# Three mixes of a four-layer graph network: from seven Winograd products in fp32 to three fp32r passes over split operands, with the SBUF pools laid out anew

## The chip, the cores and the metric

The kernel runs on one core of one Trainium2 chip. The metric is device time in microseconds (us) for one launch; before the change it is 946.98 us, the median of 3 runs (946.92 to 947.29).

## The reference

32 graphs of 512 nodes with 128 features pass four layers, each of the form `x = x + layer(relu(layernorm(x)), adj)`; `adj` is one 512 x 512 matrix for all graphs. Cut to what matters here:

```python
# layer 0: attention over the graph, from adj > 0 and a vector e (softmax by rows)
out = (A * I) @ (h @ W[0]) + (A * (1 - I)) @ (h @ W[1]) + bias
# layer 1: Chebyshev hops, the same matrix twice
x1 = einsum('bnf,nw->bwf', h, adj)                 # first mix
x2 = 2 * einsum('bnf,nw->bwf', x1, adj) - h        # second mix
out = relu(concat(h, x1, x2, x1, x2) @ Theta1 + bias)
# layer 2
feat = relu(h @ psi_w + psi_b)
msg = einsum('nm,bnd->bmd', adj * adj, feat)       # the mix of layer 2
out = relu(concat(msg, h) @ phi1_w + phi1_b) @ phi2_w + phi2_b
# layer 3: attention with tanh-clipped scores, masked by adj
out = (softmax-like of exp(8 * tanh(h q (h k)^T / (8 sqrt(128)))) * adj) @ h @ v
```

All arrays are fp32.

## The kernel before

**Tiling.** The work runs in pairs of graphs: q = 0 to 15 is a pair, b = 0 or 1 a graph in it, r = 0 to 7 a round of two pairs (A = 2r and C = 2r + 1). Nodes lie in four blocks of 128 (t, i), on the partitions; `xq` and `xt` keep all of x in SBUF from start to end.

**Mixes before.** A mix multiplies a 512 x 512 matrix with the 512 rows of a pair. It is done as one level of Winograd's form of Strassen's algorithm: the matrix is cut in 2 x 2 blocks of 256, and seven products of blocks (`products`, `ORDER`) take the place of eight. The sums of blocks on the matrix side are made once (`sum_steps`, on POOL); those on the data side for each pair (`right_steps`, L350 to L361: rt_h for layer 1's first mix, rt_w for its second, rt_feat for layer 2). `by_feature` (L384) gives the result with features on the partitions (layer 1's first mix x1T, layer 2's msgT), `by_token` (L391) with nodes on them (layer 0's mix and layer 1's second). Each product is 256 columns wide, in fp32; VectorE and ScalarE put the results together as they come out of PSUM (`mixed`, L402 to L424; `evict` in layer 1, L1031 to L1056).

**Layer 1, a round.** `normed` (ScalarE, L252) gives h; `transposed` (VectorE 32 x 32 transposes L288, then a bounce through DRAM, L295 and L297) gives hT; `straight` copies it into node order (hs, POOL, L739). The first mix gives x1T. Because Theta1's five blocks act on h, x1, x2, x1, x2, the kernel multiplies first and mixes after: p_w = h Th1 + x1 Th2 (`weighed`, L464, copied out as w by ScalarE at L987), then the second mix of w with adj, plus the "own" matmuls h Th0 (L797), bias, relu and the residual.

**Layer 2, a pair.** feat (L1092, L1093), the mix msgT, phi1 (L1109, L1110) with the relu at L1111, phi2 and the residual (L1115).

**Layer 3, a (q,b).** It already uses the three-pass form. A number v is split in a high part (v rounded on its way into an fp32r tile, scaled by `DOWN`), a low part (the rest, brought to scale) and a mid part made of v and high; high times high, low times low and mid times mid, each one fp32r matmul, sum up to the product at a known factor (`UP`, `LOW`). `moving_parts` splits keys (ScalarE L436, POOL L437, VectorE L438), `scaled_parts` queries (L442 to L444). Scores of 512 columns (L1155) go through tanh (L1156), exp (L1160) and the mask (L1162, VectorE and POOL by turns) into ex, and ex times hv (p_av, L1172) is scaled and added to x (L1174, L1177).

**Order.** Layer 0 (`round0`) is written out by hand in program order under `manual_schedule`. After it the layers are generators, and the loop at the end (`waiting`, `active`) interleaves them: each pass starts the next entry and takes one step of every generator that runs, the older first. From there the compiler orders each engine's instructions itself, with program order as priority. Stores and loads are issued on SP.

**Pools.** A tag is a set of buffers of equal size, and a tile waits for a free one. Before: "square" (const, 4 of 8 KB a partition: adj, att, attT, later x1T, sq, the mask adjTx and three ex), "sums" (2), and in `work` "rt" (6), "u" (3), "quad" (2), "hT" (4), "h" (3), and "hs" (6, in `late`); layers 0 to 3 share them by turns. In layer 3 keys take "hs" and "u", queries "rt", ex "square", and qkh with hv "quad".

Of the kernel before, what the change touches and what calls it, by code (L numbers as in the profile page):

```python
# [17 lines left out]
P = 128  # L18
QR = 32
# [10 lines left out]
def kernel(  # L30
# [48 lines left out]
    work = ctx.enter_context(tc.tile_pool(name="work", bufs=4))  # L79
    bounce = ctx.enter_context(tc.tile_pool(name="bounce", bufs=4, space=bass.MemoryType.DRAM))  # L80
# [11 lines left out]
    def square_tile(name):  # L92
        return const.tile([P, NT, N], F32, tag="square", name=name, bufs=4)
# [13 lines left out]
    adj_s = square_tile("adj_s")  # L107
# [198 lines left out]
    def sum_steps(mat, name, eng=nc.gpsimd):  # L306

        a11, a12 = mat[:, 0:2, 0:H], mat[:, 2:4, 0:H]
        a21, a22 = mat[:, 0:2, H:N], mat[:, 2:4, H:N]
        extra = const.tile([P, 3, 2, H], F32, tag="sums", name=f"sums_{name}", bufs=2)  # L310
        s1, s2, s4 = extra[:, 0], extra[:, 1], extra[:, 2]
        sums[name] = {1: a11, 2: a12, 3: s4, 4: a22, 5: s1, 6: s2, 7: a21}
        for out, op, p, q in ((s1, OP.add, a21, a22), (s2, OP.subtract, s1, a11),
                              (a21, OP.subtract, a11, a21), (s4, OP.subtract, a12, s2)):
            tc.keep_in_program_order(eng.tensor_tensor(out, p, q, op))
            yield

# [5 lines left out]
    def att_sums():  # L323
# [3 lines left out]
        extra = const.tile([P, 3, 2, H], F32, tag="sums", name="sums_att", bufs=2)  # L327
# [15 lines left out]
    def right_blocks(half, name, engs):  # L343

        right = {}
        for _ in right_steps(half, name, engs, right):
            pass
        return right

    def right_steps(half, name, engs, right):  # L350
        b11, b12, b21, b22 = half(0, 0), half(0, 1), half(1, 0), half(1, 1)
        if len(b11.shape) == 4:
            t = [work.tile([P, 2, 2, D], F32, tag="rt", name=f"rt_{name}_{i}", bufs=6) for i in range(4)]
        else:
            t = []
            for i in range(2):
                two = work.tile([P, 2, 2, D], F32, tag="rt", name=f"rt_{name}_{i}", bufs=6)
                t += [two[:, 0], two[:, 1]]
        right.update({1: b11, 2: b21, 3: b22, 4: t[3], 5: t[0], 6: t[1], 7: t[2]})
        for i, (p, q) in enumerate(((b12, b11), (b22, t[0]), (b22, b12), (b21, t[1]))):  # L360
            engs[i].tensor_sub(t[i], p, q)  # L361
            yield
# [18 lines left out]
    def by_feature(p, a, b, first):  # L381

        for k in range(2):
            nc.tensor.matmul(p[:, :H], b[:, k, :], a[:, k, :], start=(first and k == 0),  # L384
                             stop=(k == 1), skip_group_check=True)

# [8 lines left out]
    def u_tile(name):  # L395
        return work.tile([P, 2, H], F32, tag="u", name=f"u_{name}", bufs=3)

    def mixed(name, left, right, dst):

        m1 = dst[:, 0, H:], dst[:, 1, :H], dst[:, 1, H:]  # L400

        def evict(k, p):  # L402
            p = p[:, :H]
            if k == 1:
                nc.scalar.copy(m1[0], p)
            elif k == 6:
                nc.vector.tensor_add(m1[1], p, m1[0])
            elif k == 7:
                nc.vector.tensor_add(m1[2], p, m1[0])
            elif k == 5:  # L410
                return
            elif k == 2:
                nc.scalar.copy(dst[:, 0, :H], p)
            elif k == 4:
                nc.vector.tensor_add(dst[:, 0, H:], p, m1[0])
            elif k == 3:
                nc.vector.tensor_add(dst[:, 1, :H], p, m1[1])

        def evict2(k, p):
            evict(k, p)  # L420
            if k == 5:
                held.append(p)
            if k == 7:
                nc.vector.tensor_add(dst[:, 1, H:], held[0][:, :H], m1[2])  # L424

        held = []
        return products(name, by_feature, left, right, evict2)
# [40 lines left out]
    def quad_tile(name):  # L468
        return work.tile([P, 2, 2 * N + 2 * NT], F32, tag="quad", name=name, bufs=2)
# [8 lines left out]
    def project_steps(q, hT, copy=nc.scalar.copy):  # L478
        r, w = divmod(q, 2)
        if w == 0:  # L480
            if r % 3 == 2:
                g[r] = square_tile(f"g_{r}").rearrange("p t (b w f) -> p t b w f", b=2, w=2)
            else:
                t = quad_tile(f"g_{r}").rearrange("p w e -> p (w e)")[:, : 4 * N]
# [243 lines left out]
    late = ctx.enter_context(tc.tile_pool(name="late", bufs=4))  # L728
    for _ in range(NQ // 4, NQ // 2 - 1):
# [4 lines left out]
    def straight(hT, b, scale, name):  # L734

        s = late.tile([P, N], F32, tag="hs", name=name, bufs=6)
        src = hT[:, :, b, :].rearrange("p b (a c) -> p a b c", c=QR)
        if scale is None:
            nc.gpsimd.tensor_copy(split(s), src)  # L739
        else:  # L740
            nc.gpsimd.tensor_mul(split(s), src, split(scale))
# [8 lines left out]
    def late_sums():  # L750

        yield from sum_steps(adj_s, "adj")


        for out, op, p, q in ((1, OP.add, 1, 3), (2, OP.add, 2, 4), (0, OP.subtract, 0, 2)):
            tc.keep_in_program_order(nc.gpsimd.tensor_tensor(th[:, out, :], th[:, p, :], th[:, q, :], op))
            yield
        tc.keep_in_program_order(nc.gpsimd.tensor_scalar(th[:, 2, :], th[:, 2, :], 2.0, None, OP.mult))
# [493 lines left out]
```

## Time and profile before

| what | value |
|---|---|
| median of 3 runs | 946.98 us (946.92 to 947.29) |
| the profiled execution, its own time | 946.18 us |
| its span, from the first to the last instruction | 944.4 us |
| granted TensorE clock | 1.00 of full speed |
| DMA | 86.08 MB, mean 91 GB/s |

The profile is one execution. PE is TensorE's matmuls, PEld its weight loads, DVE VectorE, ACT ScalarE, POOL GpSimd, SP the queue that issues nearly all DMAs. A row of groups gives line, engine, operation, tiles and shapes, count, busy time and mean ns; a row of the timeline gives the start, the length, engine, line, tiles, count, and in brackets the idle time before it with what ended it. An fp32 matmul has two records. Ends of matmuls are modelled, so the distance between starts tells what one costs.

### The profile page before, as it was taken

The page shows a single profiled execution, that of the slowest core. Times are in us where ns is not written, and L with a number is a line of the kernel's source. Part 1 is how long each engine was busy: PE and PEld are TensorE (multiplying, and loading weights), DVE is VectorE, ACT ScalarE, POOL GpSimd, SP SyncE. Part 2 cuts the span into 40 slices and gives each one's busy share as a digit, 9 for nine tenths or more (in the row PEclk, how much of TensorE's full clock was granted, in tenths as well). Part 3 has the DMA queues.
Part 4 walks back from the last instruction along what each step waited for, and adds up shares of the span by engine and source line. Part 5 has one row for each costly group of instructions (what it writes and reads, how often), then busy time and mean ns, then how long its engine had stood idle before and what let it go on. Part 6 is the DMA issues. An engine that isn't in the chain of part 4 may idle for free. (4 is left out here: it accounts for less than half of the span.)

```text
span 944.4 us, 15678 instructions
## 1 busy us (share of the span) xinstructions
PE 929.0 (98%) x5625; PEld 811.2 (86%) x5625; DVE 685.4 (73%) x1390; ACT 499.1 (53%) x1120; POOL 543.8 (58%) x536
## 2 busy tenths in 40 slices
PE   8999999999999999999999999999989999999997
PEld 4899999899999999899977787778779899999996
DVE  8888885745555545556667766565699999999995
ACT  5864451451241242365734855545677666666663
POOL 5878997933428524421624334433467878787873
PEclk9999999999999999999999999999999999999999
DMA  9256533242341311424333342223223121212111
GB/s 260 58 157 193 166 112 90 72 131 67 87 122 60 90 32 59 134 67 112 90 112 86 93 128 77 86 68 90 67 60 98 57 79 57 79 57 78 34 35 44
DMA packets 83916, 86.08 MB, mean 91 GB/s; under 512 B 6784, under 2 KB 74624, under 8 KB 83840
## 3 DMA queue, kind: packets, MB, share of 16 engines
q1 hardware_dynamic: 83552, 84.57, 31.8%
q8 instruction: 44, 0.72, 0.3%
q10 hardware_dynamic: 288, 0.52, 0.1%
q14 instruction: 32, 0.26, 0.1%
HBM read 44.17 MB, written 40.89 MB: 90 GB/s over the span
## 5 line engine op out<-in xcount | busy, mean ns | idle before, releaser
L252 ACT ACTIVATE h<-x,sh,rs 128x128 f32<-128x128 f32 x512 | 209.5, 485 | 46.6 <-PE p_x1T_d L384 21.6
L1172 PE MATMUL p_av<-qkh_hv,ex 128*128 128x129 f32 x1024 | 121.8, 276 | 3.2 <-POOL ex L1162 2.2
L1172 PEld LDWEIGHTS p_av<-qkh_hv,ex 128*128 128x128 f32 x1024 | 119.1, 191 | 6.2 <-POOL ex L1162 3.0
L1162 POOL TENSOR_TENSOR ex<-ex,adjTx 128x512 f32<-128x512 f32 x62 | 105.0, 1713 | 6.7 <-issue 5.7
L1162 DVE TENSOR_TENSOR ex<-ex,adjTx 128x512 f32<-128x512 f32 x66 | 87.5, 1331 | 18.4 <-ACT ex L1160 18.4
L288 DVE STREAM_TRANSPOSE hb_hT<-h 128x512 f32<-128x512 f32 x120 | 82.0, 697 | 24.2 <-ACT h L252 23.9
L232 DVE BATCH_NORM_STATS2 bn<-x 128x6 f32<-128x256 f32 x248 | 89.5, 417 | 0.5
L361 POOL TENSOR_TENSOR rt_w<-w,rt_w 128x512 f32<-128x512 f32 x16 | 20.4, 1273 | 110.3 <-DVE rt_w L361 92.0
L361 POOL TENSOR_TENSOR rt_feat<-feat,feat 128x256 f32<-128x256 f32 x16 | 11.6, 725 | 119.4 <-ACT feat L1093 119.4
L1156 ACT ACTIVATE ex<-p_score 128x512 f32<-128x512 f32 x128 | 69.7, 591 | 17.7 <-PE p_score L1155 17.6
L987 ACT COPY w<-p_w 128x512 f32<-128x512 f32 x32 | 18.2, 574 | 106.1 <-PE p_w L464 106.1
L1160 ACT ACTIVATE ex<-ex 128x512 f32<-128x512 f32 x128 | 73.2, 638 | 0.8
L437 POOL TENSOR_TENSOR key_low<-hT,key_high 128x512 fp32r<-128x512 f32 x32 | 54.5, 1702 | 32.2 <-ACT key_high L436 29.7
L444 POOL TENSOR_TENSOR query_mid<-query_high,query_low 128x512 fp32r<-128x512 f32 x32 | 41.2, 1288 | 41.5 <-PE p_qkh L1139 22.2
L442 ACT ACTIVATE query_high<-qkh_hv 128x512 fp32r<-128x512 f32 x32 | 20.2, 633 | 65.0 <-DVE qkh_hv L1142 64.2
L1155 PE MATMUL p_score<-query_high,key_high 128*128 128x512 f32 x128 | 52.4, 417 | 1.9 <-ACT query_high L442 1.9
L1155 PE MATMUL p_score<-query_mid,key_mid 128*128 128x512 f32 x128 | 50.2, 396 | 0.8 <-POOL query_mid L444 0.8
L464 PE MATMUL p_w<-th,hs 128*128 128x128 f32 x256 | 49.5, 275 | 0.0
L464 PE MATMUL p_w<-th,x1T 128*128 128x128 f32 x256 | 49.5, 275 | 0.0
L1155 PE MATMUL p_score<-query_low,key_low 128*128 128x512 f32 x128 | 49.4, 390 | 0.0
L1104 POOL TENSOR_TENSOR x<-x,phi2b 128x256 f32<-128x256 f32 x64 | 45.0, 732 | 0.0
L1093 ACT ACTIVATE feat<-feat 128x512 f32<-128x512 f32 x32 | 20.1, 629 | 41.1 <-DVE feat L1092 41.1
(256 smaller groups left out, 2373.1 us busy)
## 6 DMA issues: line engine op xcount, KB each, us to landing
d_hT<-hb_hT SPq DMA_DIRECT2D x240, 128.0 KB
hT<-d_hT SPq DMA_DIRECT2D x60, 512.0 KB
x<-in_x_dram SPq DMA_DIRECT2D x32, 256.0 KB
out_dram<-x SPq DMA_DIRECT2D x31, 256.0 KB
adjT_d<-adj_squares SPq DMA_DIRECT2D x4, 256.0 KB
sq<-in_adj_dram SPq DMA_DIRECT2D x4, 256.0 KB
adjTx<-adjT_d SPq DMA_DIRECT2D x4, 256.0 KB
adj_s<-in_adj_dram ACTq DMA_DIRECT2D x2, 256.0 KB
```

The source lines that it names most:

```text
L232: nc.vector.bn_stats(st[:, k].rearrange("p e s -> p (e s)"), xt[q][:, b, t : t + 2, :].rearrange("p t f -> p f t"))
L252: nc.scalar.activation(h[:, b, t, :], xt[q][:, b, t, :], AF.Relu, bias=shift[q][:, i : i + 1], scale=scale[q][:, i : i + 1])
L288: nc.vector.transpose(hb[:, :, b].rearrange("p j t r -> p t j r"), h[:, b].rearrange("p t (j c) -> p t j c", c=QR))
L437: nc.gpsimd.tensor_sub(low, x, high.bitcast(F32))
L444: nc.gpsimd.tensor_sub(mid, high.bitcast(F32), low.bitcast(F32))
L464: nc.tensor.matmul(p[:, blk(t)], hT(t), w, start=(i == 0), stop=(i == len(terms) - 1))
L1104: tc.keep_in_program_order(nc.gpsimd.tensor_add(xi, xi, spread(phi2b, 2)))
L1155: nc.tensor.matmul(ps, keys[b][i][:, t, :], query[i], start=(i == 0), stop=(i == 2))
L1156: nc.scalar.activation(ex[:, t, :], ps, AF.Tanh, scale=UP / (8.0 * math.sqrt(D)))
L1160: nc.scalar.activation(ex[:, t, :], ex[:, t, :], AF.Exp, scale=8.0)
L1162: eng.tensor_mul(split(ex[:, t, :]), split(ex[:, t, :]), crossed(adjTx[0][:, t, :]))
L1172: nc.tensor.matmul(po[:, i, : D + 1], ex[:, t, blk(i0 + i)], hv[:, t, :], start=(t == 0), stop=(t == NT - 1))
```

## The change

The three mixes (layer 1's two and layer 2's) no longer use seven products of blocks. Both operands are split in high, low and mid, as layer 3 does, and a mix of one graph (512 columns) is 3 parts x 4 node blocks = 12 fp32r matmuls of 512 columns in one PSUM bank. `sum_steps`, `right_blocks`, `by_feature` and `mixed` are gone; layer 0's mix stays as it was.

- adj is split once, during layer 0 (`late_parts`, ScalarE and POOL); adj * adj is split on POOL during layer 1 (`square`), starting one entry of `waiting` sooner; the mask's load (`load_mask`) moves from there to the end of layer 2.
- h is split for the first mix (`split_up`), w as it leaves PSUM (`weighed`: ScalarE high, VectorE low and mid), feat for layer 2's mix. The results leave PSUM in one ScalarE copy each (`mixed_parts`).
- The second mix takes one bank per node block i: four own matmuls per bank, then the 12, then two VectorE instructions.
- Pools: layer 0's square, rt, u, quad and sums tiles lie in a pool of their own ("early"), the hd tiles in "owns"; both are closed after layer 0, and a pool "after" takes their room, with six "wide" tiles (8 KB a partition) and eleven "small" ones (2 KB). w1's three parts, the parts of adj * adj, msgT, and in layer 3 the keys (three parts in one), ex and values are wide; parts of h and feat, x1T, y, qkh and query parts are small. adj and its parts, later the mask, have a tag "matrix" of three. hs moves into the tag "hT" (4).

```diff
+    early_scope = ExitStack()
+    region0 = early_scope.enter_context(tc.tile_pool(name="early", bufs=2, side="right"))
...
+    def matrix_tile(name, dtype=F32):
+        return const.tile([P, NT, N], dtype, tag="matrix", name=name, bufs=3)
+
+    def wide_tile(name, dtype=F32):
+        return after.tile([P, 4, N], dtype, tag="wide", name=name, bufs=6)
+
+    def small_tile(name, dtype=F32):
+        return after.tile([P, N], dtype, tag="small", name=name, bufs=11)
...
+    def mixed_parts(name, left, right, dst):
+
+        p = bank(f"p_{name}")
+        for part in range(3):
+            for t in range(NT):
+                nc.tensor.matmul(p, right[part][:, blk(t)], left[part][:, t, :],
+                                 start=(t == 0 and part == 0), stop=(t == NT - 1 and part == 2))
+        nc.scalar.activation(dst, p, AF.Copy, scale=UP)
+
+    def three(name):
+        return [small_tile(f"{part}_{name}", F32R) for part in PARTS]
...
+    def late_parts():
+
+        adj_parts.extend(matrix_tile(f"adj_{part}", F32R) for part in PARTS[:2])
+        high, low = adj_parts
+        for t in range(NT):
+            nc.scalar.activation(high[:, t, :], adj_s[:, t, :], AF.Copy, scale=DOWN)
+            tc.keep_in_program_order(nc.gpsimd.tensor_sub(adj_s[:, t, :], adj_s[:, t, :], high[:, t, :].bitcast(F32)))
+            yield
...
+        nc.gpsimd.tensor_scalar(th[:, 0, :], th[:, 0, :], 1.0 / UP, None, OP.mult)
+        for t in range(NT):
+            nc.scalar.activation(low[:, t, :], adj_s[:, t, :], AF.Copy, scale=LOW)
+        yield
+        adj_parts.append(matrix_tile(f"adj_{PARTS[2]}", F32R))
...
+            hT[q] = work.tile([P, 2, N], F32, tag="hT", name=f"hs_{q}", bufs=4)
...
+        def split_up(q):
+            for b in range(2):
+                parts[q, b] = three(f"h_{q}_{b}")
+                moving_parts(h[q][:, b].rearrange("p t f -> p (t f)"), *parts[q, b])
 
         def first(q):
-            for _ in mixed(f"x1T_{q}", sums["adj"], right[q], x1T(q)):
-                pass
             for b in range(2):
-                hs[q, b] = straight(hT[q], b, None, f"hs_{q}_{b}")
+                x1[q, b] = small_tile(f"x1T_{q}_{b}")
+                mixed_parts(f"x1T_{q}_{b}", adj_parts, parts[q, b], x1[q, b])
...
         def weighed(q):
             for b in range(2):
-                p = projected(f"p_w_{q}_{b}", (columns(hs[q, b]), th[:, 1, :]), (columns(x1T(q)[:, b]), th[:, 2, :]))
-                nc.scalar.copy(w1[:, :, b, q % 2, :], p)
+                j = 2 * (q % 2) + b
+                p = projected(f"p_w_{q}_{b}", (rows(q, b), th[:, 1, :]), (columns(x1[q, b]), th[:, 2, :]))
+                high, low, mid = (tiles_of(part)[:, :, j, :] for part in w1)
+                nc.scalar.activation(high, p, AF.Copy, scale=DOWN)
+                nc.vector.tensor_sub(low, p, high.bitcast(F32))
+                nc.vector.scalar_tensor_tensor(mid, p, 1.0 / UP, high.bitcast(F32), OP.mult, OP.subtract)
...
+        w1 = [wide_tile(f"w_{part}_{r}", F32R) for part in PARTS]
...
+        for i in range(NT):
+            p = bank(f"p_l1_{r}_{i}")
+            for j in range(4):
+                nc.tensor.matmul(p[:, blk(j)], rows(2 * r + j // 2, j % 2)(i), th[:, 0, :],
+                                 start=(j == 0), stop=False, skip_group_check=True)
+            for part in range(3):
+                for t in range(NT):
+                    nc.tensor.matmul(p, adj_parts[part][:, t, blk(i)], w1[part][:, t, :],
+                                     start=False, stop=(part == 2 and t == NT - 1), skip_group_check=True)
+            y = small_tile(f"y_{r}_{i}")
+            nc.vector.scalar_tensor_tensor(tiles(y), tiles(p), UP, spread(b1, 4), OP.mult, OP.add)
+            x = xq[r].rearrange("p w b t f -> p (w b) t f")[:, :, i, :]
+            nc.vector.scalar_tensor_tensor(x, tiles(y), 0.0, x, OP.max, OP.add)
...
-        right = right_blocks(lambda J, b: feat[b][:, 2 * J : 2 * J + 2, :], f"feat_{q}", [nc.gpsimd] * 4)
+        right = [three(f"feat_{q}_{b}") for b in range(2)]
+        for b in range(2):
+            moving_parts(feat[b], *right[b])
...
-            keys[b] = [late.tile([P, NQR, P], F32R, tag="hs", name=f"key_{part}_{q}_{b}", bufs=6) for part in PARTS[:2]]
-            keys[b].append(work.tile([P, NQR, P], F32R, tag="u", name=f"key_{PARTS[2]}_{q}_{b}", bufs=3))
+            both = wide_tile(f"key_{q}_{b}", F32R)
+            keys[b] = [both[:, i].rearrange("p (t n) -> p t n", t=NQR) for i in range(3)]
...
-            ex = square_tile(f"ex_{q}_{b}")
+            ex = wide_tile(f"ex_{q}_{b}")
...
+            nc.gpsimd.tensor_mul(row, row, row)
+            nc.gpsimd.tensor_scalar(split(high), crossed(row), DOWN, 1.0, OP.mult, OP.mult)
+            yield
+            nc.gpsimd.tensor_sub(crossed(row), crossed(row), split(high.bitcast(F32)))
+            nc.gpsimd.tensor_scalar(split(low), crossed(row), LOW, 1.0, OP.mult, OP.mult)
+            yield
...
+    own_scope.close()
+    early_scope.close()
+    after = ctx.enter_context(tc.tile_pool(name="after", bufs=6, side="right", reuse_waits="tile"))
...
-    waiting[5].append(square())
+    waiting[4].append(square())
...
+    waiting[-2].append(load_mask())
```

## The prediction

> **What bounds the kernel now.** I read the page first: the busy line, the slices, the groups; then the stretches by layer, then TensorE's timeline.
>
> ```profile
> span 944.4 us, 15678 instructions
> PE 929.0 (98%) x5625; PEld 811.2 (86%) x5625; DVE 685.4 (73%) x1390; ACT 499.1 (53%) x1120; POOL 543.8 (58%) x536
> 0.00:180.00 180.00, 174.92 (x1089) 154.06 (x1090) 144.76 (x337) 97.63 (x240) 143.71 (x150) 1.00 0.50 137
> 180.00:460.00 280.00, 279.12 (x1666) 254.29 (x1666) 159.18 (x331) 110.90 (x279) 116.42 (x139) 1.00 0.33 90
> 460.00:680.00 220.00, 219.46 (x1117) 170.00 (x1117) 143.15 (x299) 115.50 (x269) 90.26 (x126) 1.00 0.32 92
> 680.00:944.00 264.00, 255.46 (x1757) 232.80 (x1756) 238.31 (x425) 175.09 (x334) 193.38 (x122) 1.00 0.20 61
> ```
>
> The four stretches are about layers 0, 1, 2 and 3 (columns: stretch, length, then PE, PEld, DVE, ACT, POOL). TensorE is full in all; in layers 1 and 2 nothing else passes 65%, in layer 3 VectorE has 238 of 264 us. Since ends of matmuls are modelled, I took starts:
>
> ```profile
> 203.22 1.03 PE L384 MATMUL p_x1T_a<-adj_s,h 128*128 128x256 f32 x4
> ...
> 209.26 1.89 PE L391 MATMUL p_l_a<-w,adj_s 128*128 128x256 f32 x8
> ...
> 775.32 3.74 PE L1172 MATMUL p_av<-qkh_hv,ex 128*128 128x129 f32 x32
> 778.82 0.47 PE L1155 MATMUL p_score<-query_high,key_high 128*128 128x512 f32 x1
> 779.13 0.39 PE L1155 MATMUL p_score<-query_low,key_low 128*128 128x512 f32 x1
> ...
> 781.44 0.40 PE L1155 MATMUL p_score<-query_mid,key_mid 128*128 128x512 f32 x1
> ```
>
> One whole mix (7 products x 4 records = 28) takes 209.26 - 203.22 = 6.04 us, 0.2157 per record of 256 columns; an fp32 matmul is two such records. In layer 3 the fp32r matmul of 512 columns is one record and starts every (781.44 - 779.13)/10 = 0.231 us; ten in an earlier run (771.23 to 773.50) give 0.227. With such spacings I laid the matmuls end to end: outside the first 20 us the gaps come to less than 21 us in all, about half of them at 680-760 and after 920. So the kernel lasts as long as TensorE's list, and a change is worth what it takes from that list, unless a wait appears.
>
> [...]2 x 0.2157 = 0.431 us for 256 columns against 0.229 for 512, a ratio of 3.8 per column. [...]key_mid on VectorE took 0.68 us at 777.00 and 1.76 at 783.93.
>
> **The change part by part.**
>
> *Matmuls.* Removed: layer 1's first mix, its second, layer 2's mix, 448 records each (the groups at L384 and L391 on adj_s, sq and their sums): 1344 x 0.2157 = 289.9 us. Added: 3 mixes x 16 pairs x 24 matmuls of 512 columns = 1152 at 0.229 = 263.8. Net -26.1 us; with 0.227 -28.4, with 0.231 -23.8. The "own" matmuls (16 of 128 columns a round) and the projections stay. All of it lies on the path.
>
> *Other engines in layers 1 and 2*, per pair. POOL, layer 1: loses four rt_h subtractions (0.75) and half of three rt_w (1.27), gains two subtractions for the low part (1.28, the query_mid row): 4.9 becomes 2.6; the two copies (0.77) stay. VectorE, layer 1: loses five adds of 0.42, half of the second mix's eviction (twelve instructions of 0.67 to 0.79 and an rt_w, 9.2 us a round); gains two key_mid-like instructions (1.14), two low at 0.69, two mid about 0.75 and half of eight evictions (0.75): 6.7 becomes 8.2. ScalarE gains two 0.63 and 0.43 of eviction. Layer 2: VectorE +0.2, ScalarE +1.7, POOL -0.4. A pair lasts about 16 us in layer 1 and 13.3 in layer 2; all lies beside the matmuls. Price 0. The cover is the next pair's mix (5.5 us) and the own matmuls (3.6): without it the chain high, low, mid behind p_w (0.57 + 0.69 + 0.75 = 2 us) would stand 8 times, 16 us.
>
> *Squares.* POOL's work on sq grows from 12.4 us to 4 x (1.15 + 1.58 + 1.70 + 1.58) + 4 x 1.27 = 29, spread over nine steps of layer 1, where POOL has 164 us idle: 0. The mask's load leaves that place for the end of layer 2: its four issues held SP 11.5 us (250.14), ahead of hT loads that layer 3 needs only steps later: 0. Three w1 parts, the raw square and two sq parts fill the six "wide" buffers, so w1 is single from there; its writers wait for the end of the last second mix, and p_w and the next first mix stand between: 0.
>
> *Layer 0.* The halves of adj cost ScalarE 5 us and POOL 8 x 1.28 + 2.3 = 12.5 against 7.0. POOL is at 16.4 to 18.1 of 20 us there; I take +1 (0 to 4).
>
> *Layer 0 to 1.* The first split of h goes into memory that layer 0 still uses, and TensorE waits for high (0.63) and then low (1.28), where rt_h lay ready. +2 (0 to 5; no gain, as nothing on this path gets shorter).
>
> *Layer 2 to 3.* The three parts of sq hold three of six wide buffers until the last layer-2 mix; keys of pair 1, now split at 660, wait for them. +2 (0 to 6).
>
> *Layer 3.* Same work, less memory. Keys (3 sets in tags "hs" and "u"), ex (3 in "square") and values (2 in "quad") had eight places; now six shared. How places are given the trace shows:
>
> ```profile
> 281.12 1.28 POOL L361 TENSOR_TENSOR rt_w<-w,rt_w 128x512 f32<-128x512 f32 x1 [17.94 <-DVE rt_w L361]
> ...
> 286.64 0.72 POOL L361 TENSOR_TENSOR rt_h<-h 128x256 f32<-128x256 f32 x1 [1.79 <-PE p_l_d L391]
> ...
> 290.39 0.68 DVE L1048 TENSOR_TENSOR y<-p_l_b,u_l 128x512 f32<-128x512 f32 x1
> ```
>
> The first rt_w place is free when product 6 ends (284.67), and POOL at 284.86, yet rt_h waits for product 5: the first place was kept for y, earlier in the program, which is written only at 290.39. So within a tag places go in program order. Per step of two (q,b) the program asks for ex(n), values, ex(n+1), key, key. Counting those alive, ex(n) gets its place only when the av of n-1 has ended (freeing ex and values), where now tanh runs 10 to 14 us ahead of that (779.8 against 793.8). The loop is then: tanh x4 2.06, exp x4 2.21 (rows at 680.58, 682.50), the same for n+1, two query highs 1.26, POOL's pair of multiplies (3.44, row at 778.78), which can start behind the second exp and so ends 2.3 after the fourth, av 3.50, five handovers of 0.1 (rt_h above began 0.08 after the end of its product, 284.67 + 1.89): 16.1 us. Behind a waiting tanh on ScalarE stand its exps and the next pairs' key and query highs; the multiplies on VectorE and POOL wait for it, and p_av for those. TensorE's own list per step is 2 x (0.69 + 0.85 + 2.77 + 3.55) = 15.7, and the measured period is 15.9 (key_high at 776.27 and 792.16). So the spare is gone: 16.1 bare, and VectorE, 15.3 busy of 15.9, must hit each handover. I take 16.5: 14 steps x 0.6 = +8. Bounds: -4 (the gaps it has now vanish) to 14 x 2.6 = +36 (a period of 18.5).
>
> *Sum.* -26.1 + 1 + 2 + 2 + 8 = -13.1 us. Against the profiled execution (946.18 us for a span of 944.4, 1.8 around it) that is 933.1; the median of the runs, 946.98, lies 0.8 higher: **934**.
>
> **Rivals.**
> *A, the whole gain.* Program order is overtaken where it matters (the scores of n run into PSUM ahead, as they can with eight banks), layer 3 keeps 15.9: -26.1 + 3 = 924. For it: TensorE's list in layer 3 is unchanged and its gaps small. Against: keys always fill their three places today. 0.27.
> *B, slower: six places for three kinds of tile in layer 3.* ex and its av alternate instead of overlapping, and TensorE waits for tanh, exp and the multiplies in each step. It decides from a period of 15.9 + 21.1/14 = 17.4 us; at 18.5 the sum is 947 - 21.1 + 36 = 962; with no overlap at all (tanh, exp, tail, av = 10.1, with three handovers 10.4 per (q,b) against 7.95) 32 x 2.45 = +78, 1004. For it: VectorE's 96% leaves no slack. 0.30.
> *C, no change*: a period near 17.4. 0.07.
> *D, that the passes are dearer elsewhere than in the scores*: from 0.25 us per matmul the gain is gone. Against: same form, new weights each time there too, other engines busier. Inside the range, no chance of its own.
>
> **How the numbers follow.** Forecast (928 to 942) 0.36, A 0.27, B 0.30, C 0.07. Faster by over 0.2% (1.9 us, about what a measurement here can tell from none): 0.36 + 0.27 = 0.63; within: 0.07; slower: 0.30. Range: below, A with the cheaper matmul and half of its three small costs, 947 - 28.4 + 1.5 = 920; above, B at 18.5 with the upper ends of the other costs in part, 966. About 0.05 lies below, 0.13 above. As both signs hold much: the forecast's own range is 928 to 942.
>
> **What would show it.** fp32r matmuls of both mixes 0.227 to 0.231 us apart (right), 0.25 (D). Layers 1 and 2 end some 21 to 26 us earlier; gaps between p_w and the second mix would show the 2 us cover missing. Layer 3's period from one av to the next but one: 15.9 (A), 16.5 (forecast), over 17.4 (B); in B TensorE idles before p_av on ex, and ScalarE's tanh starts when the av before it ends. The forecast is wrong if tanh still runs ahead (then A), or if key splits starve.

## The result and the profile after

The changed kernel takes 974.41 us (median of 4 runs, 973.47 to 975.35) against 946.98: a ratio of 1.029, 95% interval 1.027 to 1.031. It is slower by 27 us, where 934 was forecast with a range up to 966. From the page of the changed kernel, the span, the busy line and the slices of TensorE and of its clock:

```profile
span 971.3 us, 15211 instructions
PE 923.1 (95%) x5433; PEld 786.7 (81%) x5433; DVE 710.2 (73%) x1318; ACT 551.5 (57%) x1192; POOL 541.7 (56%) x461
PE   8999999996889998998999999999989999999997
PEclk9999999999798998999999999999999999999999
```

The profiled execution took 973.47 us. TensorE is busy for 6 us less than before, in a span that is 27 us longer, and its clock, full throughout before, now falls below nine tenths in slices 11, 13 and 16 (24.3 us each: 243 to 389 us). That is layer 1. The same stretches as before (stretch, length, PE, PEld, DVE, ACT, POOL, granted clock, DMA share, GB/s):

```profile
0.00:180.00 180.00, 176.01 (x1087) 153.96 (x1088) 144.89 (x337) 101.60 (x248) 147.13 (x152) 1.00 0.49 137
180.00:460.00 280.00, 247.22 (x1319) 207.59 (x1319) 155.94 (x263) 114.72 (x261) 95.51 (x83) 0.93 0.26 73
460.00:680.00 220.00, 219.13 (x1149) 172.01 (x1149) 151.03 (x261) 142.62 (x312) 96.16 (x93) 1.00 0.36 102
680.00:971.00 291.00, 280.71 (x1883) 253.12 (x1882) 258.33 (x458) 192.54 (x374) 202.87 (x136) 0.99 0.21 63
```

Only the second stretch lost something: TensorE works 247 of 280 us where it had worked 279, at a mean clock of 0.93. I cut TensorE's timeline at the same events in both traces, summed the idle time that it names in each piece, and took from narrow windows what the lowered clock cost while TensorE worked. That is an estimate, half the length of a stretch at clock 0.50: lines of four matmuls of 512 columns start 1.71 us apart there and 0.94 at full clock, a loss of 45%, which would make it 14.9 us for the 16.6 below.

| piece of TensorE's list | before | after | difference |
|---|---|---|---|
| up to the first x1T (layer 0) | 183.6 | 183.7 | +0.1 |
| to the last second mix (layer 1) | 291.4 | 328.9 | +37.5 |
| of that: idle, between instructions | 0.9 | 33.6 | +32.7 |
| of that: lost to half clock while TensorE works | 0 | 16.6 | +16.6 |
| of that: the rest | 290.5 | 278.7 | -11.8 |
| to the last msgT (layer 2) | 196.3 | 184.2 | -12.1 |
| to the end (layer 3) | 270.0 | 271.4 | +1.4 |

The sum, +26.9, is the difference of the spans. In layer 1 the clock is at half for 41.0 us in all, but for 7.7 of them TensorE stands idle anyway and loses nothing, as here (columns as above):

```profile
240.00:242.00 2.00, 0.00 (x0) 0.00 (x0) 0.00 (x0) 0.00 (x0) 0.70 (x1) 0.50 0.24 88
242.00:244.00 2.00, 0.00 (x0) 0.00 (x0) 0.00 (x0) 0.00 (x0) 1.68 (x2) 0.50 0.00 0
```

The rest still holds about 3 us of waiting: a matmul of 512 columns lasts 0.39 us by the trace, while the next follows 0.23 after its start, so each of the 20 gaps costs 0.16 us more than the idle time that is named. The work itself fell by some 15 us in layer 1. So it fell about as forecast, and waits, some 52 us with the clock's part, took it back twice over, nearly all in layer 1. A round of four graphs lasts 41.2 us there (329.09 to 370.31) where it lasted 35.1, here in the kernel before:

```profile
228.50 1.03 PE L384 MATMUL p_x1T_a<-adj_s,h 128*128 128x256 f32 x4
...
263.61 1.03 PE L384 MATMUL p_x1T_a<-adj_s,h 128*128 128x256 f32 x4
```

One such round of the changed kernel, TensorE first (start, duration; the bracket gives the idle time before and what ended it):

```profile
326.79 1.09 PE L383 MATMUL p_x1T<-adj_mid,mid_h 128*128 128x512 f32 x4
329.09 1.20 PE L383 MATMUL p_x1T<-adj_high,high_h 128*128 128x512 f32 x4 [1.20 <-ACT high_h L397]
330.96 1.75 PE L383 MATMUL p_x1T<-adj_low,low_h 128*128 128x512 f32 x4 [0.68 <-POOL low_h L398]
332.51 1.91 PE L383 MATMUL p_x1T<-adj_mid,mid_h 128*128 128x512 f32 x4
...
340.87 1.28 PE L998 MATMUL p_l<-th,hs 128*128 128x128 f32 x10
344.45 1.62 PE L1002 MATMUL p_l<-w_high,adj_high 128*128 128x512 f32 x4 [2.30 <-ACT w_high L965]
345.86 1.91 PE L1002 MATMUL p_l<-w_low,adj_low 128*128 128x512 f32 x4
```

and ScalarE in the same microseconds:

```profile
327.92 0.60 ACT L385 ACTIVATE x1T<-p_x1T 128x512 f32<-128x512 f32 x1 [2.21 <-PE p_x1T L383]
328.41 1.14 ACT L397 ACTIVATE high_h<-h 128x512 fp32r<-128x512 f32 x2
...
342.27 1.65 ACT L263 ACTIVATE h<-x,sh,rs 128x128 f32<-128x128 f32 x4 [2.39 <-POOL low_h L398]
343.82 0.57 ACT L965 ACTIVATE w_high<-p_w 128x512 fp32r<-128x512 f32 x1
```

Two mixes stand back to back there: the second pair's, up to 327.9, and the next round's first, from 329.09. The parts of h for the latter are made late. high_h itself waits for no other engine, but stands in ScalarE's queue behind the eviction of x1T, which waits for the mix to end; low_h and its neighbour follow. The second pair's p_w comes only after both mixes, so that ten records of own matmuls (1.28 us) are all that lies between it and the second mix. w_high misses that by 2.30 us, behind four normalisations that wait for an h place until low_h is through. And after most of these gaps the lines of four matmuls last 1.91 us where they last 1.09 or 1.10 otherwise (and start 1.71 us apart instead of 0.94): the clock. Windows of 2 us:

```profile
328.00:330.00 2.00, 0.91 (x4) 0.67 (x4) 0.93 (x2) 1.55 (x3) 0.89 (x1) 1.00 0.00 0
330.00:332.00 2.00, 1.32 (x5) 0.89 (x4) 1.46 (x1) 0.00 (x0) 2.00 (x2) 0.84 0.00 0
332.00:334.00 2.00, 2.00 (x6) 1.53 (x5) 0.00 (x0) 1.34 (x4) 0.62 (x1) 0.50 0.00 0
334.00:336.00 2.00, 2.00 (x8) 1.58 (x8) 0.71 (x1) 1.84 (x5) 0.00 (x0) 0.80 0.00 0
336.00:338.00 2.00, 2.00 (x14) 1.72 (x13) 0.71 (x1) 1.10 (x4) 0.00 (x0) 1.00 0.00 0
```

A third cause acts in two rounds only. square() now starts one entry sooner; on GpSimd, and on TensorE below it:

```profile
242.32 1.04 POOL L1140 TENSOR_TENSOR adj_crossed<-adj_crossed 128x512 f32<-128x512 f32 x1 [1.62 <-DMA adj_crossed<-in_adj_dram]
243.32 2.52 POOL L398 TENSOR_TENSOR low_h<-h,high_h 128x512 fp32r<-128x512 f32 x2
```

```profile
244.63 2.07 PE L383 MATMUL p_x1T<-adj_low,low_h 128*128 128x512 f32 x4 [8.15 <-POOL low_h L398]
```

The last of four multiplies waits for its DMA, low_h waits behind it, and TensorE for 8.15 us. The clock is at half for 10.2 us from 239.2 on, and TensorE works through the last 4.8 of them.

### The profile page after: what moved, and what is told of

It is laid out like the page before. It is cut to its first block, busy times and chain, and to the rows that moved or that the text cites. A ratio compares the mean times of both kernels' runs of the same rounds, so it can differ in the third digit from the quotient of the medians.

```text
span 971.3 us, 15211 instructions
## 1 busy us (share of the span) xinstructions
PE 923.1 (95%) x5433; PEld 786.7 (81%) x5433; DVE 710.2 (73%) x1318; ACT 551.5 (57%) x1192; POOL 541.7 (56%) x461
## 4 chain that ended last, share of the span: by engine, by line
PE 46%; ACT 2%; DVE 2%; POOL 1%; issue 1%; POOLq 0%; ACTq 0%; DVEq 0%
PE p_av L1118 11%; PE p_msgT L383 9%; PE p_score L1101 8%; PE p_feat L425 3%; PE p_l L425 3%; PE p_phi L1056 3%; PE p_phi L1057 3%; PE p_hv L425 2%; PE p_l L1002 2%; PE p_qkh L1086 2%; ACT h L263 1%; PE p_w L425 1%; POOL ex L1108 1%; PE p_l L998 1%; ACT ex L1102 1%
## 5 line engine op out<-in xcount | busy, mean ns | idle before, releaser
L1118 PE MATMUL p_av<-hv,ex 128*128 128x129 f32 x1024 | 122.6, 277 | 6.2 <-DVE ex L1108 4.7
L1118 PEld LDWEIGHTS p_av<-hv,ex 128*128 128x128 f32 x1024 | 120.3, 193 | 9.0 <-DVE ex L1108 5.3
L1108 POOL TENSOR_TENSOR ex<-ex,adjTx 128x512 f32<-128x512 f32 x62 | 98.8, 1616 | 33.6 <-ACT ex L1106 32.5
L398 POOL TENSOR_TENSOR low_feat<-feat,high_feat 128x512 fp32r<-128x512 f32 x32 | 51.7, 1637 | 108.7 <-ACT high_feat L397 108.7
L398 POOL TENSOR_TENSOR low_h<-h,high_h 128x512 fp32r<-128x512 f32 x32 | 53.5, 1694 | 82.5 <-ACT high_h L397 44.6
L398 POOL TENSOR_TENSOR key<-hT,key 128x512 fp32r<-128x512 f32 x32 | 55.4, 1747 | 19.3 <-ACT key L397 18.5
L399 DVE SCALAR_TENSOR_TENSOR mid_h<-h,high_h 128x512 fp32r<-128x512 f32 x32 | 35.8, 1147 | 39.9 <-ACT high_h L397 39.9
L405 POOL TENSOR_TENSOR mid_query<-high_query,low_query 128x512 fp32r<-128x512 f32 x32 | 41.7, 1303 | 28.7 <-DVE low_query L404 19.7
L1101 PE MATMUL p_score<-high_query,key 128*128 128x512 f32 x128 | 52.9, 417 | 0.8 <-ACT high_query L403 0.8
L383 PE MATMUL p_x1T<-adj_low,low_h 128*128 128x512 f32 x128 | 39.8, 437 | 14.3 <-POOL low_h L398 14.3
L1101 PE MATMUL p_score<-mid_query,key 128*128 128x512 f32 x128 | 50.2, 393 | 0.4 <-POOL mid_query L405 0.4
```

What stands on the lines that cost most here:

```text
L383: nc.tensor.matmul(p, right[part][:, blk(t)], left[part][:, t, :], start=(t == 0 and part == 0), stop=(t == NT - 1 and part == 2))
L398: nc.gpsimd.tensor_sub(low, x, high.bitcast(F32))
L405: nc.gpsimd.tensor_sub(mid, high.bitcast(F32), low.bitcast(F32))
L1101: nc.tensor.matmul(ps, keys[b][i][:, t, :], query[i], start=(i == 0), stop=(i == 2))
L1108: eng.tensor_mul(split(ex[:, t, :]), split(ex[:, t, :]), crossed(adjTx[0][:, t, :]))
L1118: nc.tensor.matmul(po[:, i, : D + 1], ex[:, t, blk(i0 + i)], hv[:, t, :], start=(t == 0), stop=(t == NT - 1))
```

## The experiments

My theory from these traces: three causes (square() ahead of low_h on GpSimd; w_high late; high_h late for want of small places), each with its share of half clock. Rivals: other shortages of places, or that the three-pass list itself is longer. All ratios below are to the kernel before on the same chip.

**Each cause alone, and all three.**

```diff
 # e1, in square()
         load_crossed(raw, adj)
         yield
+        yield
+        yield
 # e2, in layer1: the own matmuls of all four row blocks first
-        for i in range(NT):
-            p = bank(f"p_l1_{r}_{i}")
+        ps = [bank(f"p_l1_{r}_{i}") for i in range(NT)]
+        for i, p in enumerate(ps):
             for j in range(4):
...
+        for i, p in enumerate(ps):
             for part in range(3):
 # e3, in layer1
-            y = small_tile(f"y_{r}_{i}")
+            y = p
```

> square() still issues its load at the same step but idles two more steps before its first multiply, so that GpSimd's multiplies no longer stand waiting for adj_crossed ahead of low_h. Theory (three causes: GpSimd's queue blocked by the square, w_high behind the next h in ScalarE's queue, high_h late for want of small places): the 8.15 and 3.44 us gaps before low_h at 244 and 289 us go, and with them the stretches of halved TensorE clock at 250 and 298 us (10.2 and 6.8 us, worth half of that each), so about -14 to -20 us: 955 to 960. Rival 1 (only the shortage of places: w1 single, eleven small places): under 3 us, 971 or more. Rival 2 (the three-pass form itself makes TensorE's list longer): no change, 974.

> The own matmuls of all four row blocks are issued first into four banks, and only then the passes over w1: 3.6 us of matmuls stand between p_w and the first use of w_high. Theory: the five gaps of 2.3 us before w_high go, with about 1.7 us of halved clock after each, so -11 to -20 us: 954 to 963. Rival 1 (w1 single, three wide places): the gaps stay because w_high waits for places and not for ScalarE's queue: 971 or more. Rival 2 (list longer): 974.

> The second mix adds the bias in its PSUM bank and reads it from there, which frees four small places a round and holds each bank a little longer. Theory: high_h of the second pair gets its places sooner, the gaps of 1.2 and 0.68 us before it go (about six times, with halved clock where it followed): -6 to -14 us, 960 to 968. Rival (high_h is late because it stands in ScalarE's queue behind the x1T eviction, not for places): no change, 973 to 975.

> All three edits together. Theory (the three causes are all there is, and they add): layer 1's 33.6 us of gaps and about 15 us of halved clock go nearly whole, 924 to 936, below the kernel before. Rival 1 (shortage of places in w1 and h stays): 945 to 960. Rival 2 (list longer): no better than 974.

Measured: 975.3, **942.3** (0.993 to 0.996), 971.3, 943.1 us. e1 tested nothing: the scheduler put the multiplies right behind their load again, and the gap stayed, 8.03 us. e3 freed places, yet each gap of 1.20 us stayed: the first hint against my third cause. e2 gained 32.1 us where 11 to 20 were expected. Its gaps before w_high are gone (9.6 us in all), most of the half clock with them (41.0 us of it become 6.8), and the gap behind the multiplies shrank to 2.53 us, as the load was issued earlier in the new order. The gaps of 1.20 and 0.68 us remain in nearly every round:

```profile
347.46 1.20 PE L383 MATMUL p_x1T<-adj_high,high_h 128*128 128x512 f32 x4 [1.20 <-ACT high_h L397]
349.35 1.20 PE L383 MATMUL p_x1T<-adj_low,low_h 128*128 128x512 f32 x4 [0.68 <-POOL low_h L398]
...
357.70 3.74 PE L998 MATMUL p_l<-th,hs 128*128 128x128 f32 x32
```

e4, with all three edits, is no better than e2 alone, where 924 to 936 was expected.

**What holds high_h.**

```diff
 # e5 (q even) and e16 (q odd), on e2: in mixed_parts
-        nc.scalar.activation(dst, p, AF.Copy, scale=UP)
+        nc.vector.tensor_scalar(dst, p, UP, None, OP.mult)
 # e6, on e2; e9 without e2; e10 has only the second edit, on e2
-                x1[q, b] = small_tile(f"x1T_{q}_{b}")
+                x1[q, b] = h[q][:, b].rearrange("p t f -> p (t f)")
-        sooner = r == 0 or C == NQ - 1
+        sooner = True
```

> The version with the own matmuls first (942.3 us), and the evictions of x1T of each round's first pair go to VectorE, so that high_h of the second pair does not stand behind them in ScalarE's queue. It asks what the gaps of 1.20 and 0.68 us left in each round wait for. If ScalarE's queue: they go, 6 x 1.9 = 11 us, 931. If small places (at that point of the program ten of eleven are held: six parts of the first pair's h, two of its x1T, two of the last round's x1T, so the second pair's parts wait for matmuls of the first pair's mix): no change, 941 to 944.

> The version with the own matmuls first (942.3 us), and x1T is written over the h it came from (no small places of its own), with the second pair's weights computed one step sooner so that three h places still do. Same question from the other side. If small places: the gaps of 1.20 and 0.68 us before high_h and low_h of the second pair go, 6 x 1.9 us, 930 to 933. If ScalarE's queue alone: no change, 941 to 944. Risk on both: h now waits for the weights of the pair before, which could open a new gap before x1T or hT.

> The changed kernel with its own matmuls block by block, as it was, but x1T written over h and the second pair's weights one step sooner. So the next round's first mix, not the own matmuls, can stand between the second pair's p_w and the second mix. Theory (any matmuls will do as cover, what matters is that something stands there; and the parts of h have places): nearly as good as with the own matmuls first as well, 926 to 935. If the own matmuls are needed as cover: the 2.3 us gaps stay with their halved clock, 5 x 4 us more: 944 to 955.

> The version with the own matmuls first (942.3 us) and the second pair's weights one step sooner, but x1T in small places of its own. Of the two edits that together gave 926.4 us it keeps only the one that releases two small places a step earlier: eight of eleven are held then when the second pair's parts ask, so three are free where six are wanted. Theory (places, one by one): half of the gain, 932 to 938. If places come only as a whole set or the order is what matters: all of it, 926, or none, 942.

> The version with the own matmuls first (942.3 us), and the x1T evictions of each round's second pair go to VectorE; these are the ones that stand in ScalarE's queue right ahead of the late high_h (the earlier run moved the first pair's). If ScalarE's queue holds high_h: the gaps of 1.20 and 0.68 us go, about -11 us, 931. If it is memory (small places that the second pair's mix releases only as it ends): no change, 941 to 944.

Measured: e5 943.3, e6 926.4, e9 926.5, e10 **923.0** (0.973 to 0.976), e16 932.2. Taken alone, e6 looked like proof of my places; e10, which leaves x1T in small places, undid that (and came out under all three of its expected values): the sooner weights are enough, and e9 shows that the own matmuls need not come first then. e5 had moved the evictions of the wrong pair. e16 moves those that stand ahead of the late high_h, and ScalarE then makes it 0.8 us into the mix of the second pair, when not even that mix's first pass was over:

```profile
336.08 0.60 ACT L968 ACTIVATE w_high<-p_w 128x512 fp32r<-128x512 f32 x1 [0.36 <-PE p_w L428]
336.58 1.14 ACT L400 ACTIVATE high_h<-h 128x512 fp32r<-128x512 f32 x2
```

The mix ran from 335.80, and the next round's follows with no gap (from 341.51). So in such a round ScalarE's queue held high_h, not memory; that part of my theory fell. Over layer 1, 7.8 us of gaps are left of e2's 14.3. What sooner = True does is seen in e10's TensorE:

```profile
333.96 1.09 PE L383 MATMUL p_x1T<-adj_mid,mid_h 128*128 128x512 f32 x4
338.38 1.18 PE L383 MATMUL p_x1T<-adj_high,high_h 128*128 128x512 f32 x4
...
344.08 3.73 PE L998 MATMUL p_l<-th,hs 128*128 128x128 f32 x32
347.57 1.18 PE L1003 MATMUL p_l<-w_high,adj_high 128*128 128x512 f32 x4
```

p_w now stands between the two mixes (335 to 338.4) and covers high_h and low_h; the second of the mixes stands behind p_w and covers w_high. One order removes both regular gaps.

**The one edit alone, and on the kernel before.** The edit is the last of those above (sooner = True).

> The changed kernel with one edit only: the second pair's weights are computed one step sooner in every round (sooner = True), where the kernel does so in the first and last round. Own matmuls block by block, x1T in small places. If the late weights are the cause of both regular gaps (no matmuls between p_w and the second mix; two small places held a step longer): 921 to 927, like the version with the own matmuls first as well (923.0). If the own matmuls are needed as cover too: 932 to 945.

> The kernel before, with the second pair's weights one step sooner in every round; nothing of the change. If the late weights hurt only the three-pass form (whose passes need all operands at their start, where the seven products need one copy first): no gap there to close, 946 to 948. If they cost the kernel before as well: under 944, and part of the gain of the best version is not the change's.

Measured: **932.6** (0.983 to 0.987) and 944.9 (0.997 to 0.999). So one condition gives back 41.8 of the 51.4 us between the changed kernel and e10. By its time e13 falls in the range that I had set for own matmuls being needed as cover, but its trace has no gap before w_high. The regular gaps are gone, and what is left is square()'s: 5.85 and 1.34 us before low_h, and 1.9 us lost to half clock (the same estimate) behind the first. That makes most of the 8.8 us by which its layer 1 is longer than e10's:

```profile
245.90 2.08 PE L383 MATMUL p_x1T<-adj_low,low_h 128*128 128x512 f32 x4 [5.85 <-POOL low_h L398]
...
252.38 1.05 PE L998 MATMUL p_l<-th,hs 128*128 128x128 f32 x8
253.19 1.19 PE L1002 MATMUL p_l<-w_high,adj_high 128*128 128x512 f32 x4
```

In e10 the load of adj_crossed happened to be issued 4 us earlier than in the changed kernel (223.7 against 227.9), and the gap was 0.64 us. In the kernel before the same edit gains 2 us; it is no part of the change, so against a kernel before with it the three passes, with the own matmuls first as e10 has them, are worth 944.9 - 923.0 = 21.9 us.

**square()'s share.**

```diff
 # e8, on e2 with e1's two steps: both in the order of the program
-            nc.gpsimd.tensor_mul(row, row, row)
+            tc.keep_in_program_order(nc.gpsimd.tensor_mul(row, row, row))
-        nc.gpsimd.tensor_sub(low, x, high.bitcast(F32))
+        tc.keep_in_program_order(nc.gpsimd.tensor_sub(low, x, high.bitcast(F32)))
 # e11, on the changed kernel: no load, so layer 2's mix has other weights
-        load_crossed(raw, adj)
-            nc.gpsimd.tensor_mul(row, row, row)
+            nc.gpsimd.tensor_mul(row, adj_parts[0][:, i, :].bitcast(F32), adj_parts[0][:, i, :].bitcast(F32))
```

> The version with the own matmuls first (942.3 us), and GpSimd's multiplies of square() and the low_h subtractions keep the order they have in the program, two steps later; in the run that only added two steps the scheduler pulled the multiplies forward again, to just behind their load. Theory (low_h stands behind four multiplies that wait for their DMA): the gap of 2.5 us at 239 us and its halved clock go, -3 to -6 us: 936 to 939. Rival (low_h is late there as in every round, for places): the gap falls to 0.7 us only, -2 us; or the multiplies, now spread, hold up low_h in other rounds: 943 or more.

> The changed kernel, where square() takes the high part of adj, which lies ready, instead of loading adj again in the crossed order: the load is left out, and layer 2's mix has other weights, so the output is not the reference's. GpSimd's multiplies no longer wait for a DMA in front of low_h; all other work is as in the changed kernel. It prices the square's place alone. Theory: the 8.15 us gap falls to the 1.9 us of the other rounds and the halved clock behind it from 5.1 us lost to 1.7: -6.3 - 3.4, 963 to 966. If the gap came from GpSimd's amount of work and not from the DMA: no change, 972 to 976.

Measured: e8 949.9 (20 runs, 945.9 to 957.0), e11 967.4 (964.6 to 970.7). e8 closed the gap at 239 us and opened others: 6.67 us at 196, where low_h now stood behind a straight copy that waited for hT, and 4.71 at 431. In e11 the gap at 244 us fell to 0.68, but one of 6.96 opened at 282, behind fifteen instructions that square() then had in front of low_h. Both halves of my expectation were half right: the DMA makes the gap at 244, the amount of work the later one.

**The clock by itself.** Ten idle matmuls ahead of the second mix, in rounds 1 to 7 (e7) and in rounds 1 to 4, which had the gap (e14):

```diff
+            if i == 0 and r:            # e14: if i == 0 and 1 <= r <= 4
+                idle = bank(f"p_fill_{r}")
+                for t in range(10):
+                    nc.tensor.matmul(idle, adj_parts[0][:, t % NT, blk(0)],
+                                     adj_parts[0][:, t % NT, :], start=True, stop=True)
```

> The changed kernel itself (974.4 us, own matmuls block by block), with ten idle matmuls of 512 columns (2.3 us, operands long ready, result unused) ahead of the first pass over w1 in rounds 1 to 7, where TensorE sat idle 2.3 us. Nothing is removed and no wait is shortened. If the halved TensorE clock comes from the gap (each 2.3 us gap followed by 3.4 us at half clock, 1.7 us of work lost): -1.7 x 5 to 7 = 962 to 967, and the clock records stay at 1.00 in those places. If the clock has another cause (the passes themselves, their neighbours): 974 or up to 10 us more.

> The changed kernel with ten idle matmuls of 512 columns (2.3 us) ahead of the second mix in rounds 1 to 4 alone, the four that have a gap of 2.3 us there; the filling of rounds 5 to 7, where no such gap was, is left away. No wait is shortened and no work removed. If each halved stretch (3.4 us, 1.7 us of work lost) comes from the idle time just before it: the clock loss falls from 20.5 to about 10 us, as it did in the first filling run, and the time with it, 962 to 966. If the clock's loss is covered by other waits: 970 to 975.

Measured: 972.2 and 966.9. In both the half clock in layer 1 falls from 41.0 to 20.5 us, and what it costs while TensorE works, by the same estimate, from 16.6 to 6.8 us in e7 and 5.7 in e14. e7 missed its number because it also put 3 x 2.3 us where no gap was; e14, just outside its 962 to 966, gains 7.6 us with more work on TensorE and no wait shortened. So in these rounds the half clock came from idle time just ahead of it, and cost time of its own. A regular round went from 41.2 to 38.6 us: two stretches, 3.4 us of lost clock by the estimate, are gone, and some 0.5 us of gap is new. Only one of the two stretches stood behind the filled gap. The other had followed the pair of 1.20 and 0.68 us, and that pair is still there at 327 and 366 us of e14, with no half clock behind it, which the filling did not set out to do; the last section has what the traces show of such pairs.

**What was left, and layer 3.** e12 is e6 with the first pair's straight copy of hT on VectorE. e15 is e10 with one wide tile held, unused, through layer 3.

```diff
 # e12
-                nc.gpsimd.tensor_copy(split(hT[q][:, b]), ...)
+                (nc.vector if q == 0 else nc.gpsimd).tensor_copy(split(hT[q][:, b]), ...)
 # e15, at the start of layer3(0); the last av reads it
+            held_place.append(wide_tile("held_place"))
```

> The best version so far (926.4 us: own matmuls first, x1T over h, weights one step sooner) with the straight copy of the first pair's hT on VectorE, because TensorE's one gap left in layer 1 (3.42 us at 194 us, with 3.4 us lost to the halved clock behind it) ends on that copy, which stands behind five low_h subtractions on GpSimd. Theory: gap and halved clock go, -4 to -7 us: 919 to 923. Rival: something else is late there, no change, 925 to 927.

> The version with own matmuls first and weights sooner (923.0 us), where one of the six wide places is held by an unused tile from the start of layer 3 to its last av. Layers 0 to 2 are as they were. If layer 3 has a place to spare: period 15.9 us, 923 to 926. If it stands at the edge, as my +8 for six places assumed: 14 steps of 0.6 to 2.6 us, 931 to 960.

Measured: e12 922.6, as expected (e6's gap of 3.42 us is still 2.43, but the 6.8 us of half clock at it are gone). It and e10 are the best versions, 2.5% under the kernel before. e15: **999.4**, 76 us more than e10 and well over the 931 to 960 expected. Two av of e15, two (q,b) apart:

```profile
721.12 3.17 PE L1124 MATMUL p_av<-hv,ex 128*128 128x129 f32 x26 [0.64 <-POOL ex L1114]
...
741.86 3.17 PE L1124 MATMUL p_av<-hv,ex 128*128 128x129 f32 x26 [0.64 <-POOL ex L1114]
```

The period is 20.74 us with five places; the changed kernel with six has

```profile
761.84 3.73 PE L1118 MATMUL p_av<-hv,ex 128*128 128x129 f32 x32
...
777.66 3.73 PE L1118 MATMUL p_av<-hv,ex 128*128 128x129 f32 x32
```

15.82, where the kernel before had 15.92 (from 775.32):

```profile
791.24 3.74 PE L1172 MATMUL p_av<-qkh_hv,ex 128*128 128x129 f32 x32
```

Six is the last number that is enough.

## Why the prediction was wrong

**Failed: "Other engines in layers 1 and 2 ... Price 0."** The step saw the danger and named its cover, "the next pair's mix (5.5 us) and the own matmuls (3.6)". Neither stood there. For the second pair the next round's mix comes ahead of p_w, since its weights are computed one step later (the condition sooner, which the diff leaves alone), and of the own matmuls only ten of 32 records come first, since the next block's were written behind this block's passes. I had checked that cover existed in the round, not that it lay between p_w and the pass. I priced the chain at 2 us without cover, eight times, as a warning outside the sum. The gap was 2.30 in four rounds, and so the prediction's own sign for missing cover, gaps between p_w and the second mix, came true; what I had not priced at all was the other end, high_h behind an eviction in ScalarE's queue (1.20 to 1.35 in six rounds, and 0.68 for low_h in four). In e16, moving what stood ahead of it to VectorE gained 10 us (942.3 to 932.2). The kernel before tolerated the same order: it had 0.9 us of idle time in layer 1, and e17 found 2 us to gain.

**Failed: the clock, which no step had.** 16.6 of the some 52 us that waits added in layer 1 are half clock. Single gaps of 2.30 us (four), and pairs of 1.20 and 0.68 (three), were followed by half clock in the changed kernel. Each regular gap, or pair of gaps, that was so followed had 3.41 us at half clock behind it: 1.7 us more by the estimate.

**Failed: "Squares ... 0."** GpSimd's idle share (164 us) hid nothing: in its queue the multiplies that waited for a DMA stood ahead of low_h, and low_h waited with them (8.15 us on TensorE). By e13's trace this is worth about 9 us where the two other causes are gone; no run took it away cleanly.

**Right in its sum: the matmul term.** Forecast -26.1. Layer 1 of e10, without the 2.2 us of its gaps and with no half clock there, is 275.3 us long against 290.5, and layer 2's work fell by 11.6: -26.8. The parts were less good, -17.4 being forecast for layer 1's two mixes and -8.7 for layer 2's, and a pass in layer 1 costs more than the 0.229 us taken: (344.08 - 338.38) / 24 = 0.2375 in the lines of e10 above. That the errors cancel is luck. Rival A had said 924 for these passes without new waits; e10 has them without, at 923.0, some 2 us of which the same edit gains without the change.

**Wrong in size: layer 3's +8 (and +2 before it); they cost 1.4 in all.** The +1 and +2 around layer 0 came to 0.1. The mechanism was there: tanh waited for an av before it, which it never did in the kernel before. From the waits of the changed kernel in 680 to 971 us (us in all, times, longest):

```profile
ACT ex L1102 <- PE p_av L1118: 37.9, 13, 2.9
ACT key L397 <- PE p_score L1101: 24.1, 12, 2.1
```

But my loop of 16.1 us was a few tenths too long, TensorE's own list ended last, and the period stayed. Rival B had the sign right and the place wrong: six places did not cost the 18.5 us that it reckoned, and five cost 20.74, about the 2 x 10.4 that the prediction had reckoned for no overlap at all.

## What to carry to other kernels

When an operand is replaced by parts that must be made first, list in order of issue what TensorE has between the producer's last matmul and the first pass that uses a part; cover that is elsewhere in the loop counts for nothing. Then ask on each engine what the new instruction stands behind and what that waits for: here an eviction ahead of high_h on ScalarE (10 us by e16), and multiplies ahead of low_h on GpSimd (8.15 us on TensorE). A short gap on TensorE was dearer here than it looks (2.30 us, and some 1.7 more at half clock), and filling it with useful work that was already due, one call moved a step sooner, gave 41.8 us (e13), more than the 21.9 of the three passes themselves.

## What the runs showed that was not expected

The granted clock has two levels in the traces of both kernels, 1.00 and 0.50, and the halved stretches in layer 1 of the changed kernel last 3.41, 6.83 and 10.24 us (1.7, 3.4 and 5.1 us lost by the estimate). They start at 239.22, 259.70, 287.00, 304.07, 331.38, 345.03, 372.34, 385.99 and 413.30 us, which is 6, 14, 19, 27, 31, 39, 43 and 51 steps of 3.413 us after the first. What goes with a halving in this trace is TensorE's idle time summed within the step before it: 2.74 us before the first (a gap of 1.20 and the start of that of 8.15), 2.22 before 287.00 (1.20 and the start of 3.44), 2.30 or 2.31 before the four behind a single gap of 2.30, and 1.80, 1.88 and 1.76 before 331.38, 372.34 and 413.30, each behind a pair of 1.20 and 0.67 or 0.68 us. From 180 us on, no step at full clock that was followed by another at full clock had more than 1.6 us (the one from 727.30). The pair of 1.35 and 0.69 us at 449.46 and 451.35 was not followed by half clock: counted so, 1.53 us fall in one step and 0.50 in the next. e16 has a single gap of 1.91 us before 238.84 and no half clock behind it (mean granted clock 1.00 from 180 to 460 us). So gaps of the same size cost clock in one place and not in another; that it depends on where they fall in such steps is my guess from one trace, and no run was made to test it.

The two subtractions low_h on GpSimd and mid_h on VectorE, from the same tiles, mostly took longer where both ran: apart 1.26 us (243 us of the changed kernel, 2.52 for two) and 0.67 (235 us, 1.33 for two), side by side at 329 us 1.80 and 1.74 for the two low_h, 0.69 and 1.79 for the two mid_h. By 1.80 against 1.26, low_h and the passes behind it come about half a microsecond later each time, an estimate. The prediction's pair for key_mid, 0.68 and 1.76 us, does not compare alone with shared: at 777.00, where key_mid took 0.68 us, GpSimd's key_low ran too, from 776.99, and took 1.83.
